# A recurrent scan with one tanh per stream and step, and its products spread between the steps

## The chip, the cores and the metric

The kernel runs on one core of one Trainium2 chip. The metric is device time in microseconds, the median of several runs. Profiles and traces are of one execution. TensorE's matmuls are called PE, its weight loads PEld, VectorE DVE, ScalarE ACT, GpSimd POOL, and the queue that issues most DMAs SP.

## The reference

Four blocks, each an attention-like mixer and a feed-forward layer with a norm behind each, run over 8 sequences of 256 tokens with 128 features. Only the first mixer is touched here, a recurrence over time with 16 heads of 8 features and 64 states:

```python
ms = jnp.mean(jnp.square(tokens), axis=-1, keepdims=True)
x = tokens * jax.lax.rsqrt(ms + EPS) * norm_w          # (B=8, T=256, 128)
x = x.reshape(B, T, H, D)                              # H=16, D=8, S=64 states
a_t = jnp.tanh(a)                                      # (H, S, S)
def step(state, x_t):
    state = jnp.tanh(jnp.einsum('bhs,hst->bht', state, a_t)
                     + jnp.einsum('bhd,hds->bhs', x_t, b))
    mixed = jnp.einsum('bhs,hsd->bhd', state, c) + skip[None] * x_t
    return (state, mixed)
_, outs = jax.lax.scan(step, state0, xs)
return tokens + outs @ w_out.T + b_out
```

All is float32. The 256 steps depend on each other; within a step the heads and the sequences don't.

## The kernel before

`l0_attn` does this mixer. The normalized input is laid out over time: `xd` holds each token's 128 features on the partitions, with even and odd steps apart (index `u`) and each product's two heads in columns of their own (index `e`).

The 16 heads are split into two streams, `h` = 0 and 1, of eight heads each. A stream's state for one step is a slice of `states[h][...]` of 128 partitions and 64 columns, `(k=4, e=2, b=8)`: four pairs of heads `k`, the two heads of a pair in the low and the high 64 partitions. A head's state stands only in the columns `e` of its own half; the other half's columns there are zeros, set once by a memset (L188). So one matmul over 128 partitions works for two heads at once: `rhs` is 16 columns (two heads by eight sequences), `lhsT` is 32 columns of `a_sb`.

The psum tile `us[h]` takes the sums for a block of `TB` = 16 steps. Its 128 partitions are four column tiles `cols[c]` of 32: c 0 and 1 take the 64 states of the pair k = 2s, c 2 and 3 those of k = 2s + 1, with s = 0, 1 on different columns.

Per block, in the program's order:

1. The products of the inputs, b times x, for all 16 steps (L224): 32 matmuls of 128 columns, the first into each bank region with `start`.
2. The steps. For each step and stream eight matmuls of 16 columns add a times the state before (L239), then two tanh (L248) bring the sums from psum to the state: one for the low partitions, one for the high, since they write different columns `e`.
3. The products of the outputs, c times the states of the whole block (L259): 16 matmuls of 128 columns, into the bank `pm`; two vector operations for each of `u` = 0, 1 add skip times x and the two halves into `outsT` (L269, L270).

The instructions are written in this order, the framework places them on each engine and sets the semaphores; around a block's edge the matmuls of the three kinds are mixed on TensorE. The state tiles and psum banks are held for two blocks (two states per stream, four banks of `ps_s`). After the scan the output projection (L280), a residual sum and a norm follow, then the experts. Nothing else in the program runs beside the scan but loads at its beginning.

`behind(ins, other, why)` (L395), used in the new code, puts an instruction behind another in an engine's order without a semaphore.

Of the kernel before, what the change touches and what calls it, by code (L numbers as in the profile page):

```python
# [42 lines left out]
def tile_post_ln_blocks(ctx: ExitStack, tc: tile.TileContext, I, out: bass.AP):  # L43
# [10 lines left out]
    def bank(pool):  # L54
        return pool.tile([P, 512], F32, tag=pool.name, name=pool.name)
# [103 lines left out]
    def l0_attn(x):  # L159

        TB = 16
        cols = [slice(32 * c, 32 * c + 32) for c in range(4)]
        low, high = slice(0, 64), slice(64, 128)
        with ExitStack() as es:
            wp = es.enter_context(tc.tile_pool(name="l0w", bufs=1))
            wk = es.enter_context(tc.tile_pool(name="l0k", bufs=2))
            a_sb = load(wp, "L0_a")  # L170
            b_sb = load(wp, "L0_b")
            c_sb = load(wp, "L0_c")
            normw = load(wp, "L0_norm_w")
            normd = load(wp, "L0_norm_d")
            skip = load(wp, "L0_skip")
            woT = load(wp, "L0_w_outT")
            bout = load_row(wp, "L0_b_out")
            S.activation(a_sb, a_sb, AF.Tanh)

            xnT = wp.tile([P, T // 2, 2, B], F32, tag="xnT", name="xnT")  # L180
            xd = wp.tile([P, T // 2, 2, 2, B], F32, tag="xd", name="xd")
            outsT = wp.tile([P, B, T], F32, tag="outsT", name="outsT")
            states = []
            for h in range(2):
                states.append([])
                for k in range(2):
                    t = wp.tile([P, TB // 2, 2, 4, 2, B], F32, tag=f"st{h}{k}", name=f"st{h}{k}")
                    (V if h else G).memset(t, 0.0)  # L188
                    states[h].append(t)
            for g in range(NG):  # L190
                sq = wk.tile([P, 4, D], F32, tag="sq", name="sq")
                G.tensor_tensor(out=sq, in0=x[g], in1=x[g], op=ALU.mult)
                ms = lanes[g % 2].small.tile([P, 4], F32, tag="ms", name="ms")
                V.tensor_reduce(ms, sq, AX.X, ALU.add)
                r = inv_sqrt(norms[g], ms, 4, 1e-4, 1.0 / D)
                xs = wk.tile([P, 4, D], F32, tag="xs", name="xs")
                for j in range(4):
# [12 lines left out]

            ps_m = es.enter_context(tc.tile_pool(name="ps_s", bufs=4, space=bass.MemoryType.PSUM))
            prev = [None, None]
            for blk in range(T // TB):
                ts = slice(blk * TB // 2, (blk + 1) * TB // 2)
                st = [states[h][blk % 2] for h in range(2)]
                us = [
                    bank(ps_m).rearrange("p (s u t e b) -> p s u t e b", s=2, u=2, t=TB // 2, e=2)
                    for h in range(2)
                ]
                for u in range(2):  # L220
                    for h in range(2):
                        for s in range(2):
                            for c in range(4):
                                PE.matmul(  # L224
                                    us[h][cols[c], s, u].rearrange("p t e b -> p t (e b)"),
                                    lhsT=b_sb[:, u, 4 * h + 2 * s + c // 2, 32 * (c % 2) : 32 * (c % 2) + 32],
                                    rhs=xd[:, ts, u, :, :].rearrange("p t e b -> p t (e b)"),
                                    start=(u == 0 and s == 0),
                                    stop=False,
                                    skip_group_check=True,  # L230
                                )
                for t in range(TB):
                    v, u = t // 2, t % 2
                    for h in range(2):
                        if prev[h] is not None:
                            for s in range(2):
                                for c in range(4):
                                    k = 2 * s + c // 2
                                    PE.matmul(  # L239
                                        us[h][cols[c], s, u, v].rearrange("p e b -> p (e b)"),  # L240
                                        lhsT=a_sb[:, u, 4 * h + k, 32 * (c % 2) : 32 * (c % 2) + 32],
                                        rhs=prev[h][:, k].rearrange("p e b -> p (e b)"),
                                        start=False,
                                        stop=(t == TB - 1),
                                        skip_group_check=True,
                                    )
                        for e, half in enumerate((low, high)):
                            S.activation(  # L248
                                st[h][half, v, u, :, e, :].rearrange("p (s k) b -> p s k b", s=2),
                                us[h][half, :, u, v, :, :],  # L250
                                AF.Tanh,
                            )
                        prev[h] = st[h][:, v, u]

                pm = bank(lanes[blk % 2].ps)[:, : TB * 2 * B].rearrange("p (u t e b) -> p u t e b", u=2, t=TB // 2, e=2)
                for u in range(2):
                    for k in range(2):
                        for q, c in enumerate(cols):
                            PE.matmul(  # L259
                                pm[c, u].rearrange("p t e b -> p t (e b)"),  # L260
                                lhsT=c_sb[:, u, 2 * q + k, :],
                                rhs=st[q // 2][:, :, u, 2 * (q % 2) + k].rearrange("p t e b -> p t (e b)"),
                                start=(u == 0 and k == 0),
                                stop=(u == 1 and k == 1),
                                skip_group_check=True,
                            )
                for u in range(2):
                    o = outsT[:, :, blk * TB : (blk + 1) * TB].rearrange("p b (t u) -> p t u b", u=2)[:, :, u]
                    V.scalar_tensor_tensor(o, xnT[:, ts, u], skip, pm[:, u, :, 0], ALU.mult, ALU.add)  # L269
                    V.tensor_tensor(o, pm[:, u, :, 1], o, ALU.add)  # L270

            for g in range(NG):
                xb = wk.tile([P, 4, D], F32, tag="sq", name="xb")
                V.scalar_tensor_tensor(
                    xb, x[g], 2.0, bout.unsqueeze(1).to_broadcast([P, 4, D]), ALU.mult, ALU.add
                )
                ps = quarters(bank(lanes[g % 2].ps))
                for j in range(4):
                    i = 4 * g + j
                    PE.matmul(  # L280
                        ps[:, j, :],
                        lhsT=outsT[:, i // 2, (i % 2) * P : (i % 2) * P + P],
                        rhs=woT,
                        start=True,
                        stop=True,
                    )
                V.tensor_tensor(xb, ps, xb, ALU.add)
                mixed(lanes[g % 2], g, xb)
# [1097 lines left out]
```

## Time and profile before

| | us |
|---|---|
| median of three runs | 2157.67 |
| lowest and highest | 2146.89, 2164.32 |
| the profiled execution | 2149.32 |
| its span, first to last instruction | 2147.6 |
| the scan in it, first to last tanh (28.9 to 315.4) | 286.5 |
| matmuls busy in the scan | 240.1 |
| tanh busy in the scan | 196.6 |
| mean granted TensorE clock, whole span | 0.872 |
| mean granted TensorE clock in the scan | 0.69 |

The profile is one execution taken apart. A fp32 matmul leaves two records of a weight load and two of a matmul, so counts are twice the program's. A matmul's end is modelled, and busy time of TensorE is a sum of overlapping records, not work at its peak. The granted clock is a share of TensorE's full rate. The idle time given for a group is what its engine waited just before, with what ended most of it.

### The profile page before, as it was taken

Reading aid. Unit: us, or ns where it says so; the run is one execution under the profiler, and the core shown is the slowest. Engines: PE = TensorE matmul, PEld = TensorE weight load, DVE = VectorE, ACT = ScalarE, POOL = GpSimd, SP = SyncE. Lnnn points to the kernel's source line nnn. Section 1 sums busy time; section 2 is a strip of 40 time slices with the busy share of each in tenths; the row PEclk is TensorE's granted clock in tenths of the full one; section 3 lists DMA queues with packets and bytes.
Section 4 is the critical chain, followed back from the end, with each engine's and each line's share of the span. In section 5 each row is a group of like instructions: output and inputs, shape, how many; then the busy total and the mean of one; then the engine's idle time right before and its main releaser. Section 6 shows DMA issues by size and latency. Waiting matters only on the chain.

```text
span 2147.6 us, 46517 instructions
## 1 busy us (share of the span) xinstructions
PE 1785.1 (83%) x18200; PEld 1188.6 (55%) x18200; DVE 1267.9 (59%) x4476; ACT 950.8 (44%) x2385; POOL 290.4 (14%) x307
## 2 busy tenths in 40 slices
PE   5888878997899999999879762676975989998787
PEld 4666654455555544654458541554753766665564
DVE  3000016586786765689636851565667988477754
ACT  5666664372464435652333310243432554444424
POOL 1000000000000000003731067721047000000000
PEclk8666668997899999999879975798996999999958
DMA  3000006950233352235479795787731000000000
GB/s 94 5 5 5 5 4 192 270 165 0 62 96 81 87 149 75 63 82 160 119 248 315 232 274 180 237 283 226 209 91 51 1 1 1 1 6 6 1 1 11
DMA packets 186523, 219.66 MB, mean 102 GB/s; under 512 B 52896, under 2 KB 132256, under 8 KB 186304
## 3 DMA queue, kind: packets, MB, share of 16 engines
q1 hardware_dynamic: 163136, 164.24, 26.4%
q0 software_dynamic: 12800, 33.57, 5.1%
q10 hardware_dynamic: 10368, 18.88, 2.3%
q8 instruction: 143, 2.34, 0.5%
q14 instruction: 76, 0.62, 0.1%
HBM read 152.07 MB, written 64.55 MB: 101 GB/s over the span
## 4 chain that ended last, share of the span: by engine, by line
PE 60%; DVE 11%; ACT 9%; DMA 8%; POOL 6%; issue 5%; SPq 0%; ACTq 0%; POOLq 0%; DVEq 0%
PE ps_o L301 8%; PE ps_m L306 7%; PE ps_m L311 5%; ACT st L248 5%; PE ps_s L239 4%; PE ps L128 4%; PE ps L1002 3%; POOL got L586 3%; POOL placed L484 3%; PE ps L996 3%; PE ps_o L575 2%; DMA got<-in_F_w_dram,ei 2%; DMA got<-made,pl 2%; PE ps_s L224 2%; PE ps L1122 2%
## 5 line engine op out<-in xcount | busy, mean ns | idle before, releaser
L239 PE MATMUL ps_s<-st,L_a 128*32 128x16 f32 x8160 | 200.9, 206 | 45.1 <-ACT st L248 22.4
L248 ACT ACTIVATE st<-ps_s 64x32 f32<-64x32 f32 x1024 | 196.5, 192 | 92.8 <-PE ps_s L239 59.2
L308 ACT ACTIVATE h<-ps_m 128x512 f32<-128x512 f32 x196 | 116.1, 597 | 241.8 <-PE ps_m L306 222.3
L239 PEld LDWEIGHTS ps_s<-st,L_a 128*32 128x32 f32 x8160 | 159.2, 134 | 89.7 <-ACT st L248 72.3
L306 PE MATMUL ps_m<-xT,wg 128*128 128x512 f32 x384 | 197.8, 598 | 7.5 <-ACT h L308 7.5
L301 PE MATMUL ps_o<-h,wd 128*128 128x512 f32 x384 | 197.6, 599 | 7.0 <-DVE h L314 7.0
L455 POOL DMA_INDIRECT got<-in_F_w_dram,ei x32 | 30.7, 959 | 1121.4 <-DVE ei L442 971.4
L269 DVE SCALAR_TENSOR_TENSOR outsT<-xnT,L_skip,ps 128x64 f32<-128x64 f32 x32 | 10.3, 323 | 272.1 <-PE ps L259 255.5
L314 DVE TENSOR_TENSOR h<-h,bc 128x512 f32<-128x512 f32 x192 | 131.3, 686 | 45.9 <-ACT h L308 39.1
L484 POOL DMA_INDIRECT placed<-x,pl x128 | 126.3, 986 | 121.6 <-DVE pl L480 83.2
L586 POOL DMA_INDIRECT got<-made,pl x128 | 122.7, 959 | 126.3 <-DMA made<-ob 87.6
L311 PE MATMUL ps_m<-xT,wu 128*128 128x512 f32 x256 | 135.0, 609 | 4.1 <-ACT h L308 3.7
L575 PE MATMUL ps_o<-w,h 64*64 64x128 f32 x1152 | 94.0, 310 | 42.1 <-DVE h L570 29.2
L301 PEld LDWEIGHTS ps_o<-h,wd 128*128 128x128 f32 x384 | 72.1, 192 | 92.7 <-issue 62.5
L306 PEld LDWEIGHTS ps_m<-xT,wg 128*128 128x128 f32 x384 | 71.0, 191 | 91.7 <-issue 65.0
L312 DVE TENSOR_TENSOR h<-h,ps_m 128x512 f32<-128x512 f32 x132 | 90.0, 682 | 48.7 <-PE ps_m L311 43.7
L575 PEld LDWEIGHTS ps_o<-w,h 64*64 64x64 f32 x1152 | 73.7, 153 | 60.1 <-DVE h L570 41.6
L996 PE MATMUL ps<-nT,A_w 128*128 128x512 f32 x192 | 97.9, 623 | 10.1 <-DVE hT L998 7.3
L1002 PE MATMUL ps<-A_w,hT 128*128 128x128 f32 x768 | 101.1, 287 | 4.0 <-DVE hT L998 4.0
L1002 PEld LDWEIGHTS ps<-A_w,hT 128*128 128x128 f32 x768 | 95.2, 200 | 15.5 <-DVE hT L998 7.9
L565 PE MATMUL ps_m<-xg,w 128*64 128x64 f32 x1152 | 57.9, 252 | 50.2 <-DMA w<-further 22.7
L577 ACT COPY ob<-ps_o 128x512 f32<-128x512 f32 x72 | 42.2, 586 | 127.2 <-PE ps_o L575 124.9
(356 smaller groups left out, 3617.4 us busy)
## 6 DMA issues: line engine op xcount, KB each, us to landing
bc<-comb SPq DMA_DIRECT2D x128, 256.0 KB
placed<-zero SPq DMA_DIRECT2D x72, 256.0 KB
xb<-placed SPq DMA_DIRECT2D x72, 256.0 KB
made<-ob ACTq DMA_DIRECT2D x72, 256.0 KB
further<-got SPq DMA_DIRECT2D x32, 512.0 KB
w<-in_F_wg_dram SPq DMA_DIRECT2D x40, 256.0 KB
w<-in_F_wd_dram SPq DMA_DIRECT2D x40, 256.0 KB
bc<-comb SPq DMA_DIRECT2D x16, 512.0 KB
```

The lines of the kernel that those rows point to most:

```text
L239: PE.matmul(us[h][cols[c], s, u, v].rearrange("p e b -> p (e b)"), lhsT=a_sb[:, u, 4 * h + k, 32 * (c % 2) : 32 * (c % 2) + 32], rhs=prev[ ...
L248: S.activation(st[h][half, v, u, :, e, :].rearrange("p (s k) b -> p s k b", s=2), us[h][half, :, u, v, :, :], AF.Tanh,)
L301: PE.matmul(acc[g], lhsT=w, rhs=h, start=begin, stop=end, skip_group_check=True)
L306: PE.matmul(pg, lhsT=wg, rhs=xT[g], start=True, stop=True)
L308: gate = S.activation(h, pg, func).ins
L311: PE.matmul(pu, lhsT=wu, rhs=xT[g], start=True, stop=True)
L314: V.tensor_tensor(h, h, bc[:, i * GT : (i + 1) * GT], ALU.mult)
L484: i = G.indirect_dma_start(placed[h][:, :], bass.IndirectOffsetOnAxis(rw[:, j, c : c + 1], 0), x[g][:, j, :], None).ins
L575: PE.matmul(po[k, i // 2, :], lhsT=h[k, i // 2, :], rhs=wd[k, i // 2, :], start=True, stop=True)
L586: G.indirect_dma_start(got[:, c, :], None, made[g // 2][:, :], bass.IndirectOffsetOnAxis(row[g][:, j, c : c + 1], 0))
L996: PE.matmul(ph, lhsT=w1[:, f * P : (f + 1) * P], rhs=nT, start=True, stop=True)
L1002: PE.matmul(po[:, j, :], lhsT=hT[:, f, j * P : (j + 1) * P], rhs=w2[:, f, :], start=(f == 0), stop=(f == 3),)
```

## The change

Three things change in `l0_attn`.

The state gets zeros between its columns. A step's slice is now 128 columns, `(k=4, e=2, z=2, b=8)`, the state at z = 1 and zeros at z = 0, with 8 more zeros at the end of the tile (2056 columns instead of 1024, again cleared once). A recurrence matmul now takes 32 columns: read from the slice's begin they are (0, e0, 0, e1), read 8 columns on they are (e0, 0, e1, 0). Column tiles c 0 and 1 read with the shift, c 2 and 3 without. So in psum the low partitions have their sums at f = 0 and zeros at f = 1, the high partitions the other way round, and one tanh over 128 partitions and 64 columns writes the state with its zeros: 512 tanh instead of 1024.

A psum bank now holds eight steps (`HB`) of one stream instead of 16. The products of the inputs are made for half a block at a time: 32 matmuls of 64 columns, 32 times instead of 16.

The products are handed out between the steps. While half a block n runs, the products of the inputs of the next half (`inputs`) are issued two behind each stream's step, and the products of the outputs of the block before (`outputs`) one behind each step of stream 1; each is put behind the last recurrence matmul of its place by `behind`. The two vector operations follow when a block's outputs are done. The first half block's inputs stand ahead of the scan, the last block's outputs behind it. The very first step now multiplies zero states too.

```diff
-                    t = wp.tile([P, TB // 2, 2, 4, 2, B], F32, tag=f"st{h}{k}", name=f"st{h}{k}")
+                    t = wp.tile([P, TB * 4 * 32 + 8], F32, tag=f"st{h}{k}", name=f"st{h}{k}")
                     (V if h else G).memset(t, 0.0)
...
-                            for s in range(2):
-                                for c in range(4):
-                                    k = 2 * s + c // 2
-                                    PE.matmul(
-                                        us[h][cols[c], s, u, v].rearrange("p e b -> p (e b)"),
-                                        lhsT=a_sb[:, u, 4 * h + k, 32 * (c % 2) : 32 * (c % 2) + 32],
-                                        rhs=prev[h][:, k].rearrange("p e b -> p (e b)"),
...
-                        for e, half in enumerate((low, high)):
-                            S.activation(
-                                st[h][half, v, u, :, e, :].rearrange("p (s k) b -> p s k b", s=2),
-                                us[h][half, :, u, v, :, :],
-                                AF.Tanh,
-                            )
-                        prev[h] = st[h][:, v, u]
...
+            HB = TB // 2
+            def inputs(n):
+                us = [
+                    bank(ps_m).rearrange("p (t u s e f b) -> p t u s e f b", t=HB // 2, u=2, s=2, e=2, f=2)
+                    for h in range(2)
+                ]
+                def product(u, h, s, c):
+                    return PE.matmul(
+                        us[h][cols[c], :, u, s, :, c // 2, :],
+                        lhsT=b_sb[:, u, 4 * h + 2 * s + c // 2, 32 * (c % 2) : 32 * (c % 2) + 32],
+                        rhs=xd[:, n // 2 : (n + HB) // 2, u, :, :],
+                        start=(u == 0 and s == 0),
+                        stop=False,
+                        skip_group_check=True,
+                    )
...
+            def outputs(blk):
...
+                def product(u, k, q):
+                    return PE.matmul(
+                        pm[cols[q], u],
+                        lhsT=c_sb[:, u, 2 * q + k, :],
+                        rhs=st[q // 2][:, :, u, 2 * (q % 2) + k, :, 1, :],
...
+            us, todo = inputs(0)
+            for f in todo:
+                f()
+            outs, finish = [], None
+            prev = [states[h][1][:, (TB - 1) * 128 :] for h in range(2)]
+            for n in range(T):
+                t, blk = n % TB, n // TB
+                if t == 0 and blk:
+                    outs, finish = outputs(blk - 1)
+                if n % HB == 0:
+                    now, ins = us, []
+                    if n + HB < T:
+                        us, ins = inputs(n + HB)
+                for h in range(2):
+                    for s in range(2):
+                        for c in range(4):
+                            k = 32 * (2 * s + c // 2) + (0 if c // 2 else 8)
+                            last = PE.matmul(
+                                now[h][cols[c], n % HB // 2, n % 2, s].rearrange("p e f b -> p (e f b)"),
+                                lhsT=a_sb[:, n % 2, 4 * h + 2 * s + c // 2, 32 * (c % 2) : 32 * (c % 2) + 32],
+                                rhs=prev[h][:, k : k + 32],
+                                start=False,
+                                stop=(n % HB == HB - 1),
                                 skip_group_check=True,
+                            ).ins
+                    st = states[h][blk % 2]
+                    S.activation(
+                        st[:, t * 128 : t * 128 + 128].rearrange("p (k e z b) -> p k e z b", k=4, e=2, z=2)[:, :, :, 1],
+                        now[h][:, n % HB // 2, n % 2].rearrange("p s e f b -> p (s e) f b"),
+                        AF.Tanh,
+                    )
+                    prev[h] = st[:, t * 128 : t * 128 + 136]
+                    more = [ins.pop(0) for _ in range(min(2, len(ins)))]
+                    if h == 1 and outs:
+                        more.append(outs.pop(0))
+                    for f in more:
+                        behind(f().ins, last, "between two steps")
+                    if finish and not outs:
+                        finish()
+                        finish = None
```

More of the change, by code (lines that the diff above doesn't have):

```diff
@@ L211, in l0_attn @@
             ps_m = es.enter_context(tc.tile_pool(name="ps_s", bufs=4, space=bass.MemoryType.PSUM))
[L212 to L215, printed above, removed]
+            HB = TB // 2
+            def inputs(n):
                 us = [
-                    bank(ps_m).rearrange("p (s u t e b) -> p s u t e b", s=2, u=2, t=TB // 2, e=2)
+                    bank(ps_m).rearrange("p (t u s e f b) -> p t u s e f b", t=HB // 2, u=2, s=2, e=2, f=2)
@@ L218, in l0_attn @@
                     for h in range(2)
                 ]
-                for u in range(2):
-                    for h in range(2):
-                        for s in range(2):
-                            for c in range(4):
-                                PE.matmul(
[L225 to L230, printed above, removed]
-                                )
@@ L232, in l0_attn @@
[L232 to L237, printed above, removed]
-                                    k = 2 * s + c // 2
-                                    PE.matmul(
-                                        us[h][cols[c], s, u, v].rearrange("p e b -> p (e b)"),
-                                        lhsT=a_sb[:, u, 4 * h + k, 32 * (c % 2) : 32 * (c % 2) + 32],
-                                        rhs=prev[h][:, k].rearrange("p e b -> p (e b)"),
[L243 to L246, printed above, removed]
-                        for e, half in enumerate((low, high)):
-                            S.activation(
-                                st[h][half, v, u, :, e, :].rearrange("p (s k) b -> p s k b", s=2),
-                                us[h][half, :, u, v, :, :],
-                                AF.Tanh,
-                            )
-                        prev[h] = st[h][:, v, u]
@@ L255, in l0_attn @@
[L255 to L264, printed above, removed]
-                                skip_group_check=True,
-                            )
@@ L267, in l0_attn @@
[L267 to L270, printed above, removed]
+                def product(u, h, s, c):
[7 more added lines that the diff above has]
+                    )
@@ new lines, in inputs, with finish @@
+                todo = [
+                    (lambda a=(u, h, s, c): product(*a))
+                    for u in range(2) for h in range(2) for s in range(2) for c in range(4)
+                ]
+                return us, todo
+            def outputs(blk):
+                st = [states[h][blk % 2][:, : TB * 4 * 32] for h in range(2)]
+                st = [t.rearrange("p (t u k e z b) -> p t u k e z b", t=TB // 2, u=2, k=4, e=2, z=2) for t in st]
+                pm = bank(lanes[blk % 2].ps)[:, : TB * 2 * B].rearrange(
+                    "p (u t e b) -> p u t e b", u=2, t=TB // 2, e=2
+                )
+                ts = slice(blk * TB // 2, (blk + 1) * TB // 2)
+                def product(u, k, q):
[3 more added lines that the diff above has]
+                        rhs=st[q // 2][:, :, u, 2 * (q % 2) + k, :, 1, :],
+                        start=(u == 0 and k == 0),
+                        stop=(u == 1 and k == 1),
+                        skip_group_check=True,
+                    )
+                def finish():
+                    for u in range(2):
+                        o = outsT[:, :, blk * TB : (blk + 1) * TB].rearrange("p b (t u) -> p t u b", u=2)[:, :, u]
+                        V.scalar_tensor_tensor(o, xnT[:, ts, u], skip, pm[:, u, :, 0], ALU.mult, ALU.add)
+                        V.tensor_tensor(o, pm[:, u, :, 1], o, ALU.add)
+                return [
+                    (lambda a=(u, k, q): product(*a)) for u in range(2) for k in range(2) for q in range(4)
+                ], finish
@@ new lines, in l0_attn @@
+            us, todo = inputs(0)
[21 more added lines that the diff above has]
+                                stop=(n % HB == HB - 1),
+                                skip_group_check=True,
+                            ).ins
[4 more added lines that the diff above has]
+                        AF.Tanh,
+                    )
+                    prev[h] = st[:, t * 128 : t * 128 + 136]
[7 more added lines that the diff above has]
+                        finish = None
@@ L272, in l0_attn @@
+            outs, finish = outputs(T // TB - 1)
+            for f in outs:
+                f()
+            finish()
             for g in range(NG):
```

## The prediction

> **What bounds the kernel now.** I read the page's costliest groups first, then the busy times by stretch, then the chain of waits and the timeline inside two single steps.
>
> The groups say who works in the scan: 8160 records of the recurrence's matmuls (two records for each of 4080 fp32 matmuls) and 1024 tanh, two per stream and step.
>
> ```profile
> L239 PE MATMUL ps_s<-st,L_a 128*32 128x16 f32 x8160 | 200.9, 206 | 45.1 <-ACT st L248 22.4
> L248 ACT ACTIVATE st<-ps_s 64x32 f32<-64x32 f32 x1024 | 196.5, 192 | 92.8 <-PE ps_s L239 59.2
> L239 PEld LDWEIGHTS ps_s<-st,L_a 128*32 128x32 f32 x8160 | 159.2, 134 | 89.7 <-ACT st L248 72.3
> ```
>
> TensorE waits for ScalarE and ScalarE for TensorE: a loop of dependences. The stretches give its size and the clock, which changes inside every block of 16 steps (columns: us, busy time and count of PE, PEld, DVE, ACT, POOL, then the granted clock):
>
> ```profile
> 28.90:315.40 286.50, 240.05 (x9632) 193.78 (x9624) 16.45 (x60) 196.55 (x1024) 0.00 (x0) 0.69 0.02 5
> 100.87:107.70 6.83, 5.31 (x263) 4.12 (x259) 0.02 (x1) 4.75 (x26) 0.00 (x0) 1.00 0.01 2
> 107.70:117.94 10.24, 9.00 (x331) 7.14 (x333) 0.11 (x1) 6.82 (x36) 0.00 (x0) 0.50 0.03 6
> 117.94:124.77 6.83, 5.16 (x269) 4.21 (x264) 1.02 (x4) 4.76 (x25) 0.00 (x0) 1.00 0.02 5
> ```
>
> The scan takes 286.5 us, 1.12 us per step, with no other work in it: what is saved here leaves the end. Now one step at half clock (chain, then timeline) and a run of steps at full clock (timeline):
>
> ```profile
> 303.38 0.46 PE ps_s L239 x16
> 303.92 0.20 ACT st L248
> 304.13 0.20 ACT st L248
> 304.38 0.46 PE ps_s L239 x16
> ```
> ```profile
> 303.92 0.85 ACT L248 ACTIVATE st<-ps_s 64x32 f32<-64x32 f32 x4 [0.15 <-PE ps_s L239]
> 304.92 0.85 ACT L248 ACTIVATE st<-ps_s 64x32 f32<-64x32 f32 x4 [0.15 <-PE ps_s L239]
> ```
> ```profile
> 85.14 5.64 ACT L248 ACTIVATE st<-ps_s 64x32 f32<-64x32 f32 x25 [0.26 <-PE ps_s L239]
> 88.33 0.75 PE L239 MATMUL ps_s<-st,L_a 128*32 128x16 f32 x32 [0.15 <-ACT st L248]
> ```
>
> At half clock a stream's own loop is the bound: 16 records of matmul 0.46, 0.13 until the tanh starts, two tanh one behind the other, the next matmul 0.05 behind the second: 1.00 us per step. At full clock ScalarE is the bound: 25 tanh without a gap in 5.64 us, 0.226 each, four of them 0.91 per step. Sixteen steps so make 15.2 us, but a block takes 18.0. The other 2.8 us are the block's edge, where 32 products of inputs and 16 of outputs stand in a heap on TensorE and the steps wait behind them (at one edge the starts of successive steps lie up to 1.9 us apart).
>
> **What the Trainium skill says.** "TensorE: Matmul & The Clock Gate", section "What's actually happening": the array runs at half rate until a window of about 3.4 us was busy, and falls back after an idle one. The trace agrees: clock changes lie on a grid of 3.41 us, two windows full and three half in most blocks. "TensorEngine Tiling (Array Packing)", section "Key Properties": column tiles work independently. The trace agrees: near an edge one tile runs six recurrence records 53 ns apart while others still run products. "ScalarE: Activation LUTs", section "What ACT_TABLE_LOAD costs": an ACTIVATE costs 186 ns plus 0.833 per element, partitions not counting. The slope holds here (384 ns at 256 columns, 597 at 512), the constant is lower (192 ns at 32).
>
> **The change, part by part.**
>
> *Tanh.* Two of 64x32 become one of 128x64, because psum now has each half's columns beside zeros. Size: 192 + 32 x 0.833 = 219 ns; partitions don't count (64x512 took 591, 128x512 597). In a stream's loop 0.216 + 0.193 becomes 0.219: 0.19 less. ScalarE's load falls from 0.91 to 2 x 0.28 = 0.56 per step, so it is no longer the bound.
>
> *Recurrence matmuls with 32 columns instead of 16.* The trace has no such form. Records of one column tile start 32 ns apart at full clock and 53 at half with 16 columns; with 128 columns (L224) 110 and 214, so 0.83 and 1.67 ns per column. Streaming 32 columns needs 27 and 53 ns: no more than the pace that the 32-column weight load already sets. Nearest evidence that load and stream overlap and don't add: 128-column weights with 64 columns moved (L882) last as long as those with 128 moved (L862).
>
> ```profile
> L882 PE MATMUL ps<-vs,dec x64: 222/275/421, 874.5 to 1175.9; 128*128 128x64 f32 x64
> L862 PE MATMUL ps<-A_tri,zb x64: 272/275/421, 853.9 to 1169.0; 128*128 128x128 f32 x64
> ```
>
> Lower bound: pace unchanged. Upper bound: load and stream add (45 and 80 ns). I take unchanged. The last record's own length grows from 182 by 16 x 0.83 to 195 ns at full clock (214 to about 245 at half).
>
> *Products between the steps.* Inputs: 64 columns instead of 128 and twice as many, the same streaming. Per step each column tile gets one input product (2 x 55 ns full, 2 x 107 half) and in one step of four an output product (2 x 110, 2 x 214). They no longer stand in a heap, so the 2.8 us per block go, if they fit beside the loop. What is queued behind them on TensorE is the other stream's recurrence, and ScalarE waits for that. Load of a tile per step at full clock: 8 x 32 + 110 = 366 ns, 586 with an output. At half clock: 640 and 1070.
>
> *The waits.* From the third block on each tanh has a second wait, on ScalarE's own earlier write of the same state tile, paid as a separate semaphore instruction (0.062 us; steps of 0.94 became 1.00 with it). The two state tiles per stream stay, so it stays, once per tanh instead of in front of the first of two.
>
> *The loop after, full clock:* 0.050 (tanh end to first record) + 0.137 (16 records issued) + 0.195 (the last) + 0.066 + 0.062 + 0.219 = 0.729. Following four tile queues through this with the products in their order adds about 0.01 where an output's tile is late: 0.74, and 0.68 in the first two blocks. The same reckoning of the loop before gives 0.90 full and 0.99 half where the trace has 0.91 and 1.00.
>
> *The clock.* What the columns need of the whole array per step, at full clock, four tiles at a time: recurrence 32 records x 32 columns x 0.83 ns / 4 = 0.213 us, inputs 8 x 64 x 0.83 / 4 = 0.107, outputs 2 x 128 x 0.83 / 4 = 0.053, together 0.373. At 0.74 per step that is 50% of the time. I worked the same share out for every 3.41 us window of the trace before: in the scan, full clock was kept after windows with 29% to 58% and lost after 8% to 13%; half clock was left after 64% and more and kept at 56% and less. A full-clock stretch of pure steps has 12% now, which is why it falls back. After, full clock should stay; and at half clock the share would be 0.747 / 1.02 = 73%, enough to leave it. So I take full clock all through, after about 10 us of start (10 steps at 1.02 instead of 0.68: 3.4 us).
>
> *Sum.* 32 x 0.68 + 224 x 0.74 + 3.4 = 191 us against 286.5: 95.5 less. Head: 64 records of 64 columns (16 tile rounds of 107 ns, 1.7 us) instead of 3.3 us before the first tanh, one added step on zero states: about 1 us less. The state tiles' memsets double (0.94 to 1.9 us each, two on POOL, two on DVE), and POOL squares x behind them: up to 1.6 us later, hidden by the first xd scaling waiting for its DMA until 16.4 us; bounds 0 and +1.6, I take 0.5. Tail as before: the last outputs stand behind the last step.
>
> Total -96: span 2147.6 to 2051.6, own time 2149.3 to 2053; the median shown is 8.4 above the own time, so 2061.
>
> **Rivals.**
> (a) *Half clock stays.* For: the scan ran at 0.69 so far. Against: the shares above. The loop then costs 0.85 us, but the tile with an output has 1.07 us of work; following the queues 1.02 per step, up to 1.07. 256 x 1.05 = 269: 17.5 less, with the head 2140.
> (b) *The products don't land between steps,* but bunch where the order of TensorE's queue or a bank's release puts them. For: before, the queue's order mixed products and steps across edges. At full clock a half block's inputs cost 8 rounds x 2 x 55 = 0.9 us, a block's outputs 0.9: 32 x 0.9 + 16 x 0.9 = 43 us kept: 2104.
> (c) *Slower: a product between two steps holds up all tiles, not its own.* Place: every slot, since what stands behind a product is the other stream's recurrence. Price at half clock, tile rounds in a row: recurrence 8 x 53, inputs two pairs of two records of 107, output two of 214: 424 + 428 + 428 = 1.28 us per step; 256 x 1.28 = 328, 41 more: 2198. It also keeps itself at half clock: 0.747 / 1.28 is 58%, under the 64%. It decides from 1.12 us per step. For: records start in the order of the queue within a round. Against: the tile that ran 53 ns apart beside running products.
>
> **How the numbers follow.** Forecast 0.77, its own range 2040 to 2085: the second wait gone would be 14 less, load and stream adding (45 ns a round) 10 more, and the runs before differ by 17. (b) 0.10, (a) 0.08, (c) 0.05. The range 2036 to 2110 takes in (b). Within 1% (about what a measurement of this kernel can tell from no change) is 2136 to 2179. Of (a), which reaches from 2122 to 2170 (80 ns a round, 1.17 a step), 0.03 counts as faster and 0.05 as the same. So faster is 0.77 + 0.10 + 0.03 = 0.90, same 0.05, slower 0.05.
>
> **What would show it.** Right: 512 tanh of 128x64 near 219 ns; PEclk near 1.0 in the scan; steps near 0.74, scan near 190 us; ScalarE below 80% busy there. Wrong: PEclk near 0.5 (a); gaps of about 1 us every 8 steps (b); steps of 1.28 with all tiles idle behind a product (c); records of one tile 45 or 80 ns apart, if load and stream add.

## The result, and the profile after

The changed kernel takes 2179.4 us (median; 2165.5 to 2190.5) where the kernel before takes 2157.5 in runs beside it. The ratio is 1.0098, with a 95% interval of 1.0075 to 1.012: slower, by about 1%. The prediction was 2061. The profiled execution after took 2174.1 us, with a span of 2172.3 against 2147.6 before. Of these 24.7 us, 19.3 are in the scan (first tanh 29.49, end of the last 335.30, so 305.8 us against 286.5), 0.6 ahead of it, and 4.8 behind it, where the code is the same.

The page's costliest groups after (line, engine, operation, tiles, shape and count; then busy us, mean ns of one; then idle us before the group and what ended most of it):

```profile
L288 PE MATMUL ps_s<-st,L_a 128*32 128x32 f32 x8192 | 174.6, 203 | 74.4 <-issue 69.8
L288 PEld LDWEIGHTS ps_s<-st,L_a 128*32 128x32 f32 x8192 | 134.2, 112 | 113.7 <-issue 80.6
L297 ACT ACTIVATE st<-ps_s 128x64 f32<-128x64 f32 x512 | 114.0, 223 | 193.7 <-PE ps_s L288 183.0
L224 PE MATMUL ps_s<-xd,L_b 128*32 128x64 f32 x2048 | 144.6, 228 | 27.1 <-issue 23.2
```

The tanh are as predicted, 512 of 223 ns, busy 114 us instead of 196.5. But the scan grew longer, so the engines must idle more. Who waits for what has turned round: before, the recurrence's loads waited for ScalarE (72.3 us); now TensorE waits for "issue", time in which it waits for nothing that the profile can name. The waits view of the scan says the same (us in total, times, longest):

```profile
ACT st L297 <- PE ps_s L288: 183.0, 300, 2.1
PEld ps_s L288 <- issue: 80.6, 62, 1.7
PE ps_s L288 <- issue: 69.8, 58, 1.6
PEld ps_s L288 <- ACT st L297: 17.9, 86, 0.3
```

Some sixty waits of 1.2 to 1.3 us on average are an unusual form. It isn't the clock: in the stretches of after the granted clock is 0.99 over the scan (0.69 before) and 1.00 in its middle, while ScalarE is busy 37% of the time and no DMA of the kernel's data runs:

```profile
29.49:335.30 305.81, 203.90 (x10657) 161.61 (x10653) 15.34 (x57) 113.97 (x512) 0.00 (x0) 0.99 0.02 5
100.00:200.00 100.00, 65.79 (x3458) 51.03 (x3459) 5.58 (x21) 36.68 (x165) 0.00 (x0) 1.00 0.02 5
```

The timeline of ScalarE shows the steps themselves, two tanh a row:

```profile
98.17 0.46 ACT L297 ACTIVATE st<-ps_s 128x64 f32<-128x64 f32 x2 [1.36 <-PE ps_s L288]
98.91 0.46 ACT L297 ACTIVATE st<-ps_s 128x64 f32<-128x64 f32 x2 [0.28 <-PE ps_s L288]
99.64 0.46 ACT L297 ACTIVATE st<-ps_s 128x64 f32<-128x64 f32 x2 [0.28 <-PE ps_s L288]
101.61 0.44 ACT L297 ACTIVATE st<-ps_s 128x64 f32<-128x64 f32 x2 [1.50 <-PE ps_s L288]
102.34 0.46 ACT L297 ACTIVATE st<-ps_s 128x64 f32<-128x64 f32 x2 [0.29 <-PE ps_s L288]
```

Steps are 0.738 us apart, what was predicted (0.74), but about every third (83 of 255) takes over 1 us, 2.13 on average; the one in these rows takes 1.97. The timeline of all engines across one of these says where it stops:

```profile
106.79 0.15 PEld L288 LDWEIGHTS ps_s<-st,L_a 128*32 128x32 f32 x7
106.80 0.26 PE L288 MATMUL ps_s<-st,L_a 128*32 128x32 f32 x6
108.08 0.28 PE L288 MATMUL ps_s<-st,L_a 128*32 128x32 f32 x10 [1.02 <-issue]
108.08 0.17 PEld L288 LDWEIGHTS ps_s<-st,L_a 128*32 128x32 f32 x9 [1.14 <-issue]
```

TensorE stops amid the 16 records of one stream's step, whose inputs are all there: six go, the rest come 1.2 us later. Nothing else runs meanwhile. So this stop is explained neither by the data nor by a product's place. Counting TensorE's records (loads and matmuls) through the trace gives the key: of the 86 gaps over 0.3 us between the starts of neighbouring records, 82 lie at the same place of a count by 256 (the 193rd to 200th record). The DMA queue with the name "instruction" (q8) moves with them: one packet per 256 records. In the DMA view of after, from 100 to 200 us:

```profile
q8 instruction: 27, 0.44, 1.8%
```

That is 16 KB a packet, 64 bytes for each of 256 instructions, one every 3.7 us. Around the stop shown, one packet runs from 105.68 to 106.62; TensorE stops at 106.86 and goes on at 108.08; the next packet starts 1.1 us after that. Over the whole scan the mean interval of these packets is 3.69 us, and 21,505 records (one of them a semaphore's) are 84.0 packets: 84 x 3.69 = 310 us, which is the length of the scan with its first products (27.2 to 335.8). The page's queues of the whole kernel, before and then after, show that the change added nine packets:

```profile
q8 instruction: 143, 2.34, 0.5%
```
```profile
q8 instruction: 152, 2.49, 0.5%
```

Where they come from: a fp32 matmul is four TensorE instructions, two loads and two matmuls. Per block of 16 steps there were 1024 for the recurrence, 128 for the inputs and 64 for the outputs, 1216; the inputs in halves are 256, so 1344.

### The profile page after: what moved, and what is told of

It reads as the page before. It is cut to its first block, busy times and chain, and to the rows that moved or that the text cites. A ratio compares the mean times of both kernels' runs of the same rounds, so it can differ in the third digit from the quotient of the medians.

```text
span 2172.3 us, 48115 instructions
## 1 busy us (share of the span) xinstructions
PE 1754.7 (81%) x19256; PEld 1156.4 (53%) x19256; DVE 1268.4 (58%) x4476; ACT 868.6 (40%) x1873; POOL 292.5 (13%) x307
## 4 chain that ended last, share of the span: by engine, by line
PE 60%; DVE 10%; DMA 10%; issue 8%; POOL 6%; ACT 4%; SPq 1%; POOLq 0%; ACTq 0%; DVEq 0%
PE ps_o L345 8%; PE ps_m L350 7%; PE ps_s L288 5%; PE ps_m L355 5%; PE ps L128 4%; POOL placed L528 3%; POOL got L630 3%; PE ps L1046 3%; PE ps L1040 2%; PE ps_s L224 2%; DMA got<-in_F_w_dram,ei 2%; DMA got<-made,pl 2%; PE ps L250 2%; PE ps L1166 2%; PE ps_o L619 2%
## 5 line engine op out<-in xcount | busy, mean ns | idle before, releaser
L288 PE MATMUL ps_s<-st,L_a 128*32 128x32 f32 x8192 | 174.6, 203 | 74.4 <-issue 69.8
L288 PEld LDWEIGHTS ps_s<-st,L_a 128*32 128x32 f32 x8192 | 134.2, 112 | 113.7 <-issue 80.6
L297 ACT ACTIVATE st<-ps_s 128x64 f32<-128x64 f32 x512 | 114.0, 223 | 193.7 <-PE ps_s L288 183.0
L224 PE MATMUL ps_s<-xd,L_b 128*32 128x64 f32 x2048 | 144.6, 228 | 27.1 <-issue 23.2
L250 PE MATMUL ps<-st,L_c 128*32 128x128 f32 x512 | 93.7, 275 | 4.3 <-issue 4.3
```

What stands on the lines that cost most here:

```text
L224: return PE.matmul(us[h][cols[c], :, u, s, :, c // 2, :], lhsT=b_sb[:, u, 4 * h + 2 * s + c // 2, 32 * (c % 2) : 32 * (c % 2) + 32], rhs=x ...
L250: return PE.matmul(pm[cols[q], u], lhsT=c_sb[:, u, 2 * q + k, :], rhs=st[q // 2][:, :, u, 2 * (q % 2) + k, :, 1, :], start=(u == 0 and k = ...
L288: last = PE.matmul(now[h][cols[c], n % HB // 2, n % 2, s].rearrange("p e f b -> p (e f b)"), lhsT=a_sb[:, n % 2, 4 * h + 2 * s + c // 2, 3 ...
```

## The experiments

**Theory A, supply:** TensorE's program comes in packets of 256 instructions, on average no faster than one per about 3.65 us; a long stage lasts at least its TensorE instructions / 256 x 3.65. **Theory B, spreading:** the products between the steps hold up the steps, by their place on TensorE. Some experiments ran on other chips, on which the kernel before takes 2326 or 2329 us instead of 2157, so only ratios to it, taken on the same chip, and lengths of the scan are compared. The three kernels that were profiled on two chips had scans that differ by 0.1 to 2.5 us between them.

### One part alone, and more instructions

`e1_heap` keeps the single tanh and puts the products back in heaps (1344 instructions per block):

```diff
-                    more = [ins.pop(0) for _ in range(min(2, len(ins)))]
-                    if h == 1 and outs:
-                        more.append(outs.pop(0))
+                    more = []
+                    if h == 1 and n % HB == HB - 1:
+                        more, ins = ins, []
+                    if h == 1 and t == 0:
+                        more, outs = more + outs, []
```

> The change without its spreading: one tanh and zeros stay, but the 32 products of a half block's inputs stand together behind the half block's last step, and the 16 products of outputs behind the first step of the next block. Theory A (TensorE's program arrives in blocks of 256 instructions, one in 3.7 us, and the scan takes as long as its blocks): 1344 instructions a block of steps as in the changed kernel, so the same time, 2170 to 2190, and still stops of 1.2 to 1.8 us every 256 records. Theory B (a product between two steps holds up the steps behind it): the stops of 1.2 us between steps go, some 84 of them, against edges as before, 2100 to 2150.

`e2_spread` spreads the products as the change does, but keeps before's state tiles, two tanh and inputs for 16 steps at a time (1216):

```diff
-                    prev[h] = st[:, t * 128 : t * 128 + 136]
-                    more = [ins.pop(0) for _ in range(min(2, len(ins)))]
...
+                    prev[h] = st[:, v, u]
+                    more = [ins.pop(0)] if ins else []
```

> The spreading alone, on the kernel before: two tanh, 16 columns, a bank of 16 steps; one product of inputs (128 columns) behind each stream's step, one of outputs behind each step. Theory A: 1216 instructions a block of steps, as before, so the time of before, 2145 to 2170. Theory B: the hold-ups come with the spreading, so slower than before by at least what the changed kernel lost, 2175 or more. The prediction's own reckoning (edges gone, 0.91 to 1.00 a step): 45 less than before, 2115.

`e6_pad` is the change with two more matmuls per stream's step, one column of zeros each, so that sums stay as they are (1600):

```diff
+                    more += [
+                        lambda c=c, h=h: PE.matmul(
+                            now[h][cols[c], n % HB // 2, n % 2, 0, 0, 1 - c // 2, :1],
+                            lhsT=a_sb[:, 0, 0, :32],
+                            rhs=prev[h][:, 0:1],
...
+                        for c in range(2)
+                    ]
```

> The changed kernel with two more matmuls behind each stream's step, each of one zero column added to psum: 4 instructions each, 4096 in the scan, with next to no work for the array. Theory A: 16 more blocks of 256 at 3.7 us, 59 more, 2225 to 2245. Theory B and any theory of the array's work: a pass of one column costs less than a recurrence's (32 ns), on two of four column tiles and beside the wait for the tanh: 0 to 20 more, 2180 to 2200.

`e10_half_inputs` is the change without the input products of s = 1, one product behind each stream's step (1216):

```diff
-                    for u in range(2) for h in range(2) for s in range(2) for c in range(4)
+                    for u in range(2) for h in range(2) for s in range(1) for c in range(4)
```

> The changed kernel with half of the products of inputs left out (those of s = 1), so that it issues 1216 instructions a block of steps like the kernel before; one product behind each stream's step instead of two. Theory A (supply of 256 instructions in 3.65 us): 8 blocks of 256 less, 29 us less than the changed kernel, so 0.995 to 1.000 of the kernel before. If the array's work or the hold-ups set the time, the steps of 0.74 stay as they are and the stops shrink in number but not by blocks: 1.005 to 1.010.

The four, with the change and before (records are TensorE's, with one to three of semaphores; before and the change were profiled on another chip than the four):

| | instructions per block of 16 steps | records of the scan | mean interval of packets, us | first to last tanh, us | ratio to before (95%) |
|---|---|---|---|---|---|
| before | 1216 | 19,395 | 3.81 | 286.5 | |
| e2_spread | 1216 | 19,395 | 3.64 | 274.2 | 0.9994 (0.9974 to 1.0013) |
| e10_half_inputs | 1216 | 19,457 | 3.69 | 278.2 | 1.0012 (0.9992 to 1.0032) |
| e1_heap | 1344 | 21,505 | 3.63 | 302.6 | 1.0139 (1.0108 to 1.017) |
| the change | 1344 | 21,505 | 3.69 | 305.8 | 1.0098 (1.0075 to 1.012) |
| e6_pad | 1600 | 25,601 | 3.65 | 361.0 | 1.0342 (1.0304 to 1.0379) |

The interval stays at 3.63 to 3.69 us while the count goes from 76 to 100 packets and the arrangement changes. The 16 packets more of e6 than of e1, on one chip, cost 58.4 us: 3.65 each, though the added matmuls stream one column. e10 takes away work together with instructions, and e6 adds instructions with next to no work: both follow the count (e10's ratio lies a little above the 0.995 to 1.000 expected, its scan is 27.6 us shorter than the change's where 29 were expected). B falls twice: with the products in heaps again (e1) the scan is only 3 us shorter, not by what the stops take, and spreading alone (e2) makes nothing slower.

Two tanh a step or one makes little difference at the same count (e2 274.2, e10 278.2), and neither does the clock: e1's scan, at 0.76, is about as long as that of the change, at 0.99, with the same count. The stretches of e1, then e2:

```profile
29.70:332.32 302.62, 218.41 (x10652) 181.04 (x10648) 16.39 (x60) 103.90 (x512) 0.00 (x0) 0.76 0.02 5
```
```profile
28.30:302.50 274.20, 242.51 (x9632) 163.31 (x9624) 15.63 (x57) 195.86 (x1024) 0.00 (x0) 1.00 0.02 5
```

The stops are where the loop outruns the supply. In e6 the waits of the recurrence for "issue" grow to the largest of any run, and 97 of its 99 gaps over 0.3 us lie at that same place of the count by 256:

```profile
PEld ps_s L288 <- issue: 97.8, 65, 2.1
PE ps_s L288 <- issue: 90.8, 64, 2.0
```

In e2, ScalarE runs without a gap between stops (timeline of ScalarE), so the 0.91 us a step predicted for two tanh at full clock are there, and the stops take back what the vanished heaps gave:

```profile
102.46 3.21 ACT L288 ACTIVATE st<-ps_s 64x32 f32<-64x32 f32 x14 [1.11 <-PE ps_s L278]
106.00 3.13 ACT L288 ACTIVATE st<-ps_s 64x32 f32<-64x32 f32 x14 [0.33 <-PE ps_s L278]
```

The kernel before is at 3.81 us per packet, just slower than the supply. Most of its gaps over 0.3 us lie at all places of the count, every 32 records, as the steps come. But its five longest in the scan, 0.69 to 1.12 us, all lie at the place of the stops, and the waits of its scan have a few for issue:

```profile
PEld ps_s L239 <- issue: 4.2, 10, 1.0
```

So it already stopped for instructions now and then, and had 3 to 5% left until it would do so throughout.

The packets' times show what the 3.65 us consist of. In the scan of the change (medians), a packet starts 1.13 us after TensorE has gone on at the place of the stops, takes 1.10 us, and TensorE goes on at the next such place 1.38 us after it has landed: 3.61 together. Between two stops TensorE gets through its 256 records faster than that (2.24 us ahead of the stop shown), so the limit isn't a cost of each instruction. In the wide kernel below (e12), which doesn't stop, a packet also starts only after that place of the count has been passed, 0.2 to 1.1 us later, but it has landed 2.7 us or more before TensorE comes to the next one. It looks as if one packet is asked for at a time, and only when TensorE has entered a new stretch of 256 records. That is read from the order of events; no run changed it.

### Fewer instructions

The other way to test A is to ask for less. A matmul over 64 output partitions in place of two over 32 halves the count, with the same sums. `e4_wide` does it for the recurrence and the inputs, one input product behind each stream's step; the outputs stay at 32 (704 per block):

```diff
-                        us[h][cols[c], :, u, s, :, c // 2, :],
-                        lhsT=b_sb[:, u, 4 * h + 2 * s + c // 2, 32 * (c % 2) : 32 * (c % 2) + 32],
+                        us[h][(low, high)[c], :, u, s, :, c, :],
+                        lhsT=b_sb[:, u, 4 * h + 2 * s + c, :],
...
-                        for c in range(4):
-                            k = 32 * (2 * s + c // 2) + (0 if c // 2 else 8)
+                        for c in range(2):
+                            k = 32 * (2 * s + c) + (0 if c else 8)
```

> The changed kernel with recurrence and input products over 64 partitions of psum instead of 32 (half as many matmuls, the same work, output products as they are). Theory A: 704 instructions a block of steps instead of 1344, 44 blocks of 256 in the scan, 163 us of supply, which is under the loop; the loop then is the bound: about 0.80 a step for a longer issue of four rounds of 64 columns, 205 us, 2070 to 2095. Theory B: products stay between the steps, 2160 to 2190. If a change between 64 and 32 columns of the array costs a drain, the steps are longer than 1 us and it is 2130 or more.

`e7_wide_heap` is that with a block's outputs in a heap, once per block:

```diff
-                    if h == 1 and outs:
-                        more.append(outs.pop(0))
+                    if h == 1 and t == 0:
+                        more, outs = more + outs, []
```

> Recurrence and input products over 64 partitions (704 instructions a block of steps), input products between the steps, output products (32 partitions) together behind the first step of the next block. The run with outputs between the steps had 0.75 a step in its first block, where there are no outputs, and 1.115 behind it. If that is the drain between 64 and 32 columns, twice per step, it is now paid twice per block: 16 x 0.75 + about 1.5 = 13.5 us a block, 215 us, 70 less than before: 0.97 of its time. If it is the work of the output products themselves, they cost the same here and the ratio stays near 1.00.

`e8_wide_all` is e4 with the outputs over 64 partitions too, their weights set beside zeros in a tile `c_wide` that the kernel fills at its start:

```diff
-                        pm[cols[q], u],
-                        lhsT=c_sb[:, u, 2 * q + k, :],
+                        pm[(low, high)[q // 2], u],
+                        lhsT=c_wide[:, u, 2 * q + k, :],
```

> As the run above, but the output products too over 64 partitions (weights with zeros beside them, made on the chip), one behind each step: no switch between 64 and 32 columns anywhere in the scan. If the switch cost the 0.37 us per step: 0.75 to 0.80 a step, 192 to 205 us, 80 to 95 less than before, 0.96 of its time. If the output product's own length did: about 1.1 a step and 1.00.

`e9_wide_two_tanh` makes all three wide in e2, so with two tanh and inputs for 16 steps (640):

```diff
-                            for c in range(4):
-                                k = 2 * s + c // 2
+                            for c in range(2):
+                                k = 2 * s + c
```

> The kernel before (two tanh, 16 columns, bank of 16 steps), with all products of the scan over 64 partitions and spread between the steps: 640 instructions a block of steps, so supply is out of the way, and only the single tanh is missing against the run with all at 64. Expected: ScalarE bound, 4 x 0.227 = 0.91 a step, 233 us, 50 less than before: 0.977. The single tanh is then worth 0.91 minus the step of the run above, some 0.13 x 256 = 33 us.

| | instructions per block | packets in the scan | first to last tanh, us | ratio to before (95%) |
|---|---|---|---|---|
| e4_wide | 704 | 44 | 280.1 | 1.0025 (1.0006 to 1.0043) |
| e7_wide_heap | 704 | 44 | 223.6 | 0.9891 (0.9846 to 0.9936) |
| e8_wide_all | 704 | 44 | 213.2 | 0.9631 (0.9592 to 0.967) |
| e9_wide_two_tanh | 640 | 40 | 254.1 | 0.989 (0.9856 to 0.9925) |

With 44 packets the supply would need 161 us and is out of the way: the stops at every 256th record are gone in all four. e4 nonetheless gained nothing, against the 0.96 to 0.97 that was hoped for: its steps, 0.75 us in the first block, which has no outputs to make, are a constant 1.115 from the second on, until the last eight, with no inputs left to make, take 0.92. The timeline of TensorE's matmuls in one step of e4 shows why:

```profile
150.38 0.22 PE L224 MATMUL ps_s<-xd,L_b 128*64 128x64 f32 x1
150.53 0.41 PE L250 MATMUL ps<-st,L_c 128*32 128x128 f32 x2
150.87 0.43 PE L288 MATMUL ps_s<-st,L_a 128*64 128x32 f32 x8
```

Between the last wide record and the first narrow one lie 0.15 us, and from the second narrow one, at 150.67, to the next wide one another 0.20. The Trainium skill, "TensorEngine Tiling (Array Packing)", section "Key Properties", says that a change of tiling mode drains TensorE; the trace agrees: in e8, without a change, the same two gaps are 0.06 and 0.04 us. (The profile puts the 0.20 down to a tanh, but the one that this stream needs had ended 0.36 us before.) Here the pair of changes with the output product between them costs 0.31 us a step (1.115 against the 0.81 of e7's steps without outputs); the product alone is a small part of it, as e8's steps show below. e7 pays for the changes once per block: one step of 1.86 us, the next ones 0.81 (timeline of ScalarE):

```profile
97.54 0.57 ACT L297 ACTIVATE st<-ps_s 128x64 f32<-128x64 f32 x2 [0.23 <-PE ps_s L288]
99.40 0.57 ACT L297 ACTIVATE st<-ps_s 128x64 f32<-128x64 f32 x2 [1.29 <-PE ps_s L288]
100.21 0.57 ACT L297 ACTIVATE st<-ps_s 128x64 f32<-128x64 f32 x2 [0.24 <-PE ps_s L288]
```

e8 has no change of tiling and spreads everything: 0.81 us a step, 0.91 in every fourth. It takes 0.963 of the time of the kernel before. And against e9, on the same chip, it gives the single tanh's worth (with the zeros and the smaller banks that belong to it) where the supply doesn't bind: 254.1 - 213.2 = 40.9 us of the scan, where 33 were expected, since e9's steps take 0.98 us and not 0.91. In e9 ScalarE is the bound, 29 tanh in one row without a gap (timeline):

```profile
96.89 7.04 ACT L294 ACTIVATE st<-ps_s 64x32 f32<-64x32 f32 x29
```

### All three on one chip

The change, the wide kernel and the kernel before, none altered, on a chip where before takes 2159 us:

> The changed kernel unaltered, to have its scan on the same chip as the wide one. Supply in blocks of 256 instructions: 84 blocks at 3.63 to 3.70 us each, 305 to 311 us from first to last tanh, and 1.009 to 1.014 times the kernel before. Spreading as the cause (the rival): the scan's length would not follow the count of blocks here; no number of its own.

> The wide kernel (all scan matmuls over 64 output partitions, 704 instructions a block of 16 steps) a second time. Supply: 44 blocks in the scan, fewer than the loop's own time allows for, so no stops, scan 210 to 216 us and 0.96 to 0.97 times the kernel before. If the first run's gain behind the scan (some 25 us more than kernels with the same code there) belonged to that chip and not to the program, the ratio is 0.970 to 0.975 and the time behind the last tanh is that of the two other kernels of this call.

> The kernel before, unaltered, to see its scan and what lies behind it on this chip. Supply: 75.75 blocks at 3.63 to 3.80 us, 275 to 288 us. Behind the last tanh: the same as for the changed kernel within 10 us if the code there alone sets it; 20 us or more apart if where the blocks of the instruction supply fall, or what the scan leaves in the queues, matters.

| | scan, us | behind it, us | span, us | ratio (95%) |
|---|---|---|---|---|
| e13_before_again | 285.1 | 1841.8 | 2155.7 | |
| e11_after_again | 308.3 | 1844.1 | 2182.0 | 1.008 (1.0056 to 1.0103) |
| e12_wide_all_again | 213.3 | 1842.0 | 2084.2 | 0.9623 (0.9556 to 0.969) |

The change's ratio is a shade below the 1.009 expected, with 84 packets at 3.71 us. Here the time behind the scan is the same for all three within 2.3 us, so nearly the whole difference between the spans is the scan: 23.2 of the change's 26.3 us, and 71.8 of the wide kernel's 71.5 (the ratio expected for that case, 0.970 to 0.975, was reckoned too high: 71.8 of 2156 is 3.3%). The wide kernel's scan, whose waits and stretch are these, has no wait for issue left in it worth naming:

```profile
ACT st L303 <- PE ps_s L294: 75.5, 259, 2.0
PEld ps L330 <- issue: 0.3, 2, 0.2
```
```profile
28.87:242.16 213.29, 213.29 (x5573) 207.54 (x5571) 15.36 (x57) 114.76 (x512) 0.00 (x0) 1.00 0.02 4
```

What stays open: on the two other chips the time behind the scan differed from program to program, from 1994 us (e8) to 2037 (e7), with the same code there. No run tells why. Where ratio and scan don't match (e7, whose scan alone would give about 0.973, most of all; the other seven by 0.2 to 0.7%), the rest presumably lies there; the kernel before was not profiled on those chips.

## Why the prediction was wrong, step by step

- **Tanh 219 ns, 512 of them:** right, 223.
- **The loop at 0.74 us, 0.68 in the first two blocks:** right, 0.738 and 0.678 between stops. (In the reading of the loop before at half clock the parts add to 1.05 us, not 1.00: the records run for 0.41 us, 303.38 to 303.79, not 0.46. The sum doesn't use it.) With it go the pace unchanged at 32 columns (records of one column tile still start 32 ns apart) and the second wait, which stayed at 0.06.
- **Full clock through the scan:** right, 0.99. That it follows from spreading the matmuls is shown by e1, which has heaps again and 0.76. The share of 50% behind it did not come, though: with the stops a step takes 1.19 us on average, so the 0.373 us of columns are 31%, near the low end of the 29% to 58% that kept full clock before. That it was enough is in part luck. Nor was the bound of 64% sharp: one window of the trace before (at 295.4 us) left half clock with 57%.
- **A product holds up its own tile only (rival c for the other):** right so far as the step of 0.738 holds both products; c's steps of 1.28 did not come. The forecast time of c, 2198, was near for another reason.
- **"They no longer stand in a heap, so the 2.8 us per block go, if they fit beside the loop":** this is the step that failed. The fit was worked out for each column tile's time and for the array's columns (50%), and not for TensorE as one reader of one program. By that account a block needs 1344 x 3.69 / 256 = 19.4 us, where the loop wants 16 x 0.74 = 11.8. In the sum, the term for the scan was 191 and measured 305.8; the stops are the 115 us between (83 steps, each 1.39 longer than the 0.74). e2 shows the same for the heaps' removal alone: a scan of 274 us, some 12 shorter than before's on another chip, in place of the 45 that 2.8 per block make.
- **"64 columns instead of 128 and twice as many, the same streaming":** true of streaming, and counted as free for that reason. It is 128 instructions more per block, 8 packets in the scan, and it is what turned no gain into a loss: with the inputs' count halved, e10 is level with before (1.0012).
- **Rival (b), bunching every 8 steps:** the stops are about three steps apart and fall amid a step's records, so it was not this.
- **Head and tail:** the first tanh was 0.6 us later, where 0.5 earlier was expected: the first products took about 1 us less, as forecast, but began 1.6 us later (27.2 against 25.6), which the prediction had as its upper bound. The tail took 4.8 us longer, which was not expected; in the pair on one chip it was 2.3.

The trace before had the numbers that were missed. The Trainium skill, "Runtime: NRT & Kernel Launch", section "Instruction fetch mechanics", says that instructions come in blocks of 16 KiB, 256 of them, by the engine's own queue, and calls the cost of a boundary mostly hidden. The size agrees with the packets here; the cost doesn't: up to 115 us of a scan of 306. Before, a packet came every 3.81 us, the shortest interval anywhere in that trace was 3.23, and TensorE's longest gaps in the scan stood at one place of the count by 256: that was the hint.

## What to carry to other kernels

Where TensorE does many small matmuls, count its instructions per stage (four for a fp32 matmul, as records show) and hold 14.4 ns for each, 3.69 / 256, against the time that the stage is to take; if the count wins, ask for fewer, larger matmuls; no kernel here came clearly under it. Equal streaming is not equal cost: a matmul split in two costs twice the instructions. A stop of TensorE with "issue" as the releaser, amid a group whose inputs are there, is to be read together with the instruction queue's packets.

## What was not expected of the hardware

- TensorE's program was supplied at no better than 3.63 to 3.71 us per 256 instructions on average in every kernel that outran it, 3.2 at the shortest, with a packet's own transfer taking 0.9 to 1.5 us. Between a packet's landing and TensorE's going on lay 1.45 us in the stop shown. Why the next packet isn't asked for earlier no run tells.
- Going from 64-partition to 32-partition output tiles and back, with one output product between, cost 0.31 us in a step of 1.115.
- A loop over 64 output partitions is slower per step than the one over 32 where no stop falls (0.81 against 0.74; loads of 137 ns mean against 112), and still wins, since it has no stops.
